# A graph layer and a mixture-of-experts encoder layer on one core: how the attention weights are turned, and how the values' experts are summed

## Chip, cores, metric

The kernel runs on one core of a Trainium2 chip. The metric is the device time of one execution in microseconds. All times below are of the kernel before the change.

## What is computed

The reference is two layers with residuals. The first is a graph convolution over 1250 nodes and 40000 edges. The second is the one that the change touches: a transformer layer over the 1250 nodes with width D = 1024, H = 16 heads of P = 64, and E = 8 experts of which K = 2 are chosen per node and head.

```python
def _gate(x, Wsel):
    s = sigmoid(einsum('bsd,hed->bhse', x, Wsel))
    _, idx = top_k(s, K)
    return s * one_hot(idx, E).sum(-2)

q = rope(einsum('bsd,hdp->bhsp', x, Wq))
k = rope(einsum('bsd,hdp->bhsp', x, Wk))
v = einsum('bsd,bhse,hedp->bhsp', x, _gate(x, Wsel_v), Wv)
att = softmax(einsum('bhsp,bhtp->bhst', q, k) / sqrt(P), axis=-1)
o = einsum('bhst,bhtp->bhsp', att, v)
out = einsum('bhsp,bhse,hepd->bsd', o, _gate(x, Wsel_o), Wo)
```

After it come a layer norm, a feed-forward of 512, and a second layer norm.

## The kernel before

Every fp32 factor is split into a rounded part and a remainder (names ending in hi and lo, or _h and _l), and a product is three matmuls, `dot` at L139 to L141. Nodes are cut into NT = 10 tiles of KT = 125.

The stages in order of time:

- **Graph layer**, 0 to about 314 us. Its normalized output z is turned by `transposed` (L165 to L175) into `zT`, with width on the partitions.
- **Queries and keys**, about 314 to 600 us. `queries_keys` makes, for each of 16 heads, three pieces of columns (L584 scales, L586 to L589 rotate, L590 and L591 split), and writes the split head to DRAM, `kq_d` (L594 the keys, L596 the queries): six DMAs per head on SP's queue. The gates' ten tiles are interleaved. Here a scheduler orders all engines.
- **Values and attention**, about 600 to 2016 us. From here the order of PE's instructions is that in which the code is written; the other engines' is the scheduler's. `values` makes, for head h and tile t, a 125 x 512 product of all eight experts (24 matmuls, with a `yield` after every six), multiplies by the gate on the DVE (L717, `ve`), sums the experts with a reduction (L720, `v`), and splits (L722 on ACT, L723 on POOL). `attention` is a second generator, stepped once in seven of eight yields of `values`. It works by chunks of 256 queries; 16 heads x 5 chunks = 80 chunks.
- **Outputs**, about 2016 to 2890 us. `outputs` loads o (`oc`, L736) and the gates (`gb`, L741), multiplies (L745), splits (L748, L750), multiplies with Wo, and adds to `acc` (L765). The last chunks of attention are stepped beside its beginning.
- **Feed-forward**, to the end.

A chunk of attention has, for each half of 128 queries: queries loaded by POOL's queue (L629), scores `s` of 128 x 1254 by six matmuls (L634), the negated maximum `most` on the DVE (L637), three exponentials on ACT with sums (L642), the total, its reciprocal and the scaling of `p` on the DVE (L645 to L647). Then, five times per chunk, `split`: four PE transposes against the identity turn two tiles of 125 keys into PSUM (L655), ACT rounds them to `att_hi` (L657), and the DVE subtracts to get `att_lo` (L659). `product` multiplies the two with the values (L670, four matmuls of 256 columns for each `split`), and at the end of a chunk o goes out through L676, L677 and L680. Products stand two splits behind.

Weights come through `weights` (L123 the load on SP, L127 the rounding on ACT, L129 the remainder on POOL). The rounded pairs lie in a ring of five slots, the raw blocks in two. SP's queue issues in order, and so does POOL's.

The buffers that matter: `s` one buffer of three PSUM banks, `mm` and `tr` two banks each, `p` five buffers, `q` four, `v2` three, `oc` two.

Of the kernel before, what the change touches and what calls it, by code (L numbers as in the profile page):

```python
# [11 lines left out]
F32 = mybir.dt.float32  # L12
# [10 lines left out]
N = 1250  # L23
# [13 lines left out]
CUT = NZ * KT  # L37
# [33 lines left out]
def gnn_ffn_kernel(  # L71
# [31 lines left out]
    o_d = [dram.tile([P, N], F32, name=f"o_d{j}") for j in range(NP)]  # L103
    g_d = dram.tile([P, N], F32, name="g_d")
# [61 lines left out]
    def transposed(hi, lo, c0, y, psum_tile):  # L166

        for half in range(2):
# [4 lines left out]
            to = (slice(None), slice(4 * half, 4 * half + 4), slice(c0, c0 + KT))  # L173
            nc.scalar.copy(hi[to], p)
            nc.vector.tensor_tensor(lo[to], p, hi[to].bitcast(F32), ALU.subtract)  # L175
# [8 lines left out]
    with ExitStack() as gctx:  # L184
# [16 lines left out]
        with ExitStack() as bctx:  # L201
# [3 lines left out]
            with tc.tile_pool(name="ring1t", bufs=6) as r1:  # L205
                ring += [r1] * 6

                def prepare(t):
# [10 lines left out]
                    transposed(yh, yl, 0, y[:KT], lambda shape: ps.tile(shape, F32, name="tr2", bufs=2))  # L219
# [274 lines left out]
        zT = [[zpool.tile([P, ND, CUT], F32R, name=f"zT0{k}") for k in range(2)]]  # L494
        for t in range(2, NT):
            new = sums([t])
            if t - 2 < NZ:
                transposed(zT[0][0], zT[0][1], KT * (t - 2), zs.pop(0)[:KT], side_bank)
                zs += new
# [5 lines left out]
    def z_of(t, d):  # L505

        k = t if t < NZ else t - NZ
        return [part[:, d, KT * k : KT * (k + 1)] for part in zT[t >= NZ]]

    def rest_of_z():  # L510

        for t in range(NZ, NT):
            z = raws[0].tile([P, D], F32, name="w_raw")[:KT]
            move(z, z_d[t])
            transposed(zT[1][0], zT[1][1], KT * (t - NZ), z, side_bank)
# [3 lines left out]
    def gates(wpool, tmp):  # L519
# [5 lines left out]
        wide = [KT, 2 * H, NX]  # L525
        order = first_wins[:KT, None, :].to_broadcast(wide)

        def pick(chosen, v, m):

            nc.vector.tensor_reduce(m, v, AX.X, ALU.max)  # L530
# [5 lines left out]
        for t in range(NT):  # L536
            p = side_bank([KT, 2 * P])
# [3 lines left out]
            s, a, b, c = (tmp.tile([KT, 2 * H, NX], F32, name=k) for k in ("s", "a", "b", "chosen"))  # L541
            m = tmp.tile([KT, 2 * H], F32, name="m")
# [5 lines left out]
            nc.vector.tensor_tensor(gate_v[:KT, t, :].rearrange("p (h e) -> p h e", h=H), s[:, :H, :], c[:, :H, :],  # L548
                                    ALU.mult)
            nc.vector.tensor_tensor(a[:, H:, :], s[:, H:, :], c[:, H:, :], ALU.mult)  # L550
            pg = psums[-1].tile([P, KT], F32, name="po", bufs=1)
            nc.tensor.transpose(pg, a[:, H:, :].rearrange("p h e -> p (h e)"), ident[:KT, :KT])
            nc.scalar.copy(gT[:, KT * t : KT * (t + 1)], pg)
# [4 lines left out]
    def queries_keys(tab, work):  # L558
# [9 lines left out]
        chunks = [(0, 0, CUT), (1, 0, 376), (1, 376, N - CUT - 376)]  # L568
# [48 lines left out]
    def attention(pool):  # L617
# [46 lines left out]
        def product(h, c, k, parts):  # L664
# [8 lines left out]
            if k + 2 < NT:  # L673
                return
# [252 lines left out]
```

## Time and profile before

| | us |
|---|---|
| median of 3 runs | 3137.41 (3130.07 to 3139.82) |
| profiled execution, its own time | 3137.92 |
| its span, first to last instruction | 3136.1 |
| around the span | 1.8 |
| PE busy | 3023.9 |
| DVE busy | 1957.2 |
| ACT busy | 1098.1 |
| POOL busy | 702.2 |
| PE's weight loads busy (beside the matmuls) | 2554.4 |

A row of the instruction groups reads: line, engine, operation, output<-input, shapes, xcount, then busy us and mean ns of one, then the engine's idle time just before these and who ended it. Matmuls are pipelined, so the mean ns of one is longer than the distance to the next; distances are read from the timeline. A row of the table by stage reads: stretch, its length, then for each engine busy us and number of instructions, the granted TensorE clock, the share of the DMA engines' time and GB/s.

### The profile page before, as it was taken

The page shows a single profiled execution, that of the slowest core. Times are in us where ns is not written, and L with a number is a line of the kernel's source. Part 1 is how long each engine was busy: PE and PEld are TensorE (multiplying, and loading weights), DVE is VectorE, ACT ScalarE, POOL GpSimd, SP SyncE. Part 2 cuts the span into 40 slices and gives each one's busy share as a digit, 9 for nine tenths or more (in the row PEclk, how much of TensorE's full clock was granted, in tenths as well). Part 3 has the DMA queues.
Part 4 walks back from the last instruction along what each step waited for, and adds up shares of the span by engine and source line. Part 5 has one row for each costly group of instructions (what it writes and reads, how often), then busy time and mean ns, then how long its engine had stood idle before and what let it go on. Part 6 is the DMA issues. An engine that isn't in the chain of part 4 may idle for free. (4 is left out here: it accounts for less than half of the span.)

```text
span 3136.1 us, 41143 instructions
## 1 busy us (share of the span) xinstructions
PE 3023.9 (96%) x15618; PEld 2554.4 (81%) x15618; DVE 1957.2 (62%) x3477; ACT 1098.1 (35%) x2472; POOL 702.2 (22%) x570
## 2 busy tenths in 40 slices
PE   6989899999999999999999999899999999999998
PEld 5777889888888888888888888787777777777787
DVE  7965687566666666666666666664444444444685
ACT  5762323234444444444444444431112112111222
POOL 2000334322222122222212222202112112112223
PEclk9999999999999999999999999999999999999999
DMA  3116555612221121222112122434333333333212
GB/s 111 60 41 190 167 142 160 167 43 52 54 55 37 42 52 47 54 55 53 43 39 53 46 54 54 102 94 123 106 85 98 96 85 103 90 82 109 75 41 92
DMA packets 151825, 254.86 MB, mean 81 GB/s; under 512 B 14521, under 2 KB 111801, under 8 KB 151458
## 3 DMA queue, kind: packets, MB, share of 16 engines
q1 hardware_dynamic: 103934, 210.68, 23.9%
q0 software_dynamic: 45824, 31.22, 5.2%
q10 hardware_dynamic: 1860, 10.24, 1.1%
q8 instruction: 124, 2.03, 0.3%
q14 instruction: 83, 0.68, 0.1%
HBM read 200.25 MB, written 56.96 MB: 82 GB/s over the span
## 5 line engine op out<-in xcount | busy, mean ns | idle before, releaser
L129 POOL TENSOR_TENSOR w_lo<-w_raw,w_hi 128x1024 fp32r<-128x1024 f32 x148 | 372.3, 2525 | 1078.0 <-ACT w_hi L127 1069.6
L141 PE MATMUL mm<-w_hi,go_lo 128*125 128x512 f32 x1280 | 507.6, 399 | 24.6 <-DVE go_lo L750 24.5
L139 PE MATMUL mm<-w_hi,go_hi 128*125 128x512 f32 x1280 | 509.5, 398 | 8.8 <-ACT go_hi L748 7.9
L139 PE MATMUL mm<-w_hi,zT 128*125 128x512 f32 x1280 | 508.4, 397 | 4.6 <-ACT raw L584 4.6
L140 PE MATMUL mm<-w_lo,go_hi 128*125 128x512 f32 x1280 | 509.9, 398 | 0.0
L140 PE MATMUL mm<-w_lo,zT 128*125 128x512 f32 x1280 | 507.1, 396 | 0.1
L141 PE MATMUL mm<-w_hi,zT 128*125 128x512 f32 x1280 | 507.1, 396 | 0.0
L642 ACT ACTIVATE p<-s,most 128x416 f32<-128x416 f32 (+1 forms) x480 | 286.0, 605 | 332.8 <-DVE most L637 329.2
L765 DVE TENSOR_TENSOR acc<-acc,mm 125x512 f32<-125x512 f32 x320 | 217.4, 683 | 163.1 <-PE mm L141 163.1
L659 DVE TENSOR_TENSOR att_lo<-tr,att_hi 125x512 fp32r<-125x512 f32 x400 | 262.6, 685 | 88.7 <-ACT att_hi L657 88.6
L141 PEld LDWEIGHTS mm<-w_hi,go_lo 128*125 128x125 f32 x1280 | 239.9, 187 | 93.6 <-DVE go_lo L750 33.7
L748 ACT CAST go_hi<-gb 128x500 fp32r<-128x500 f32 x160 | 98.2, 614 | 602.2 <-PE mm L140 600.6
L657 ACT CAST att_hi<-tr 125x512 fp32r<-125x512 f32 x400 | 235.1, 589 | 179.0 <-PE tr L655 176.0
L139 PEld LDWEIGHTS mm<-w_hi,go_hi 128*125 128x125 f32 x1280 | 239.9, 187 | 68.3 <-ACT go_hi L748 8.2
L745 DVE TENSOR_TENSOR gb<-gb,oc 128x500 f32<-128x500 f32 x160 | 103.8, 690 | 303.0 <-DMA gb<-g_d 301.8
L141 PEld LDWEIGHTS mm<-w_hi,zT 128*125 128x125 f32 x1280 | 238.3, 186 | 60.5
L140 PEld LDWEIGHTS mm<-w_lo,go_hi 128*125 128x125 f32 x1280 | 239.7, 187 | 58.4
L637 DVE TENSOR_REDUCE most<-s 128x1 f32<-128x1254 f32 x160 | 234.2, 1464 | 81.0 <-PE s L634 80.6
L655 PEld LDWEIGHTS tr<-ident,p 128*125 128x125 f32 x1600 | 234.9, 187 | 53.6 <-DVE att_lo L659 18.6
L139 PEld LDWEIGHTS mm<-w_hi,zT 128*125 128x125 f32 x1280 | 239.1, 187 | 41.0 <-ACT raw L584 4.9
L140 PEld LDWEIGHTS mm<-w_lo,zT 128*125 128x125 f32 x1280 | 239.6, 187 | 36.5 <-POOL w_lo L129 0.4
L655 PE MATMUL tr<-ident,p 128*125 128x128 f32 x1600 | 242.0, 274 | 10.2 <-DVE att_lo L659 8.1
(201 smaller groups left out, 5166.6 us busy)
## 6 DMA issues: line engine op xcount, KB each, us to landing
gb<-g_d SPq DMA_DIRECT2D x160, 250.0 KB
w_raw<-in_wv SPq DMA_DIRECT2D x64, 512.0 KB
w_raw<-in_wo SPq DMA_DIRECT2D x64, 512.0 KB
q<-kq_d POOLq DMA_DIRECT2D x160, 128.0 KB, 2.6
kq_d<-qk_hi SPq DMA_DIRECT2D x48, 312.5 KB
kq_d<-qk_lo SPq DMA_DIRECT2D x48, 312.5 KB
k<-kq_d POOLq DMA_DIRECT2D x16, 625.0 KB, 4.4
oc<-o_d SPq DMA_DIRECT2D x80, 125.0 KB
```

The source lines that it names most:

```text
L129: (lo_engine or nc.gpsimd).tensor_tensor(lo, raw, hi.bitcast(F32), ALU.subtract)
L139: nc.tensor.matmul(p, lhsT=lhs[0], rhs=rhs[0], start=start, stop=False)
L140: nc.tensor.matmul(p, lhsT=lhs[0], rhs=rhs[1], start=False, stop=False)
L141: nc.tensor.matmul(p, lhsT=lhs[1], rhs=rhs[0], start=False, stop=stop)
L637: nc.vector.tensor_reduce(most, s[:, :, :KW], AX.XY, ALU.max, negate=True)
L642: nc.scalar.activation(p[:, k0 : k0 + n], s[:, k, :n], AF.Exp, bias=most, accum_out=parts[:, k : k + 1])
L655: nc.tensor.transpose(t[:, j, P * i : P * (i + 1)], p[:, KT * (k + j) : KT * (k + j + 1)], ident)
L657: nc.scalar.copy(hi, t)
L659: nc.vector.tensor_tensor(lo, t, hi.bitcast(F32), ALU.subtract)
L745: nc.vector.tensor_tensor(gb[:, :, mine], gb[:, :, mine], o[:, None, mine].to_broadcast([P, 4, KT]), ALU.mult)
L748: copied = nc.scalar.copy(hi, gb[:, :, mine])
L765: nc.vector.tensor_tensor(acc[t][:, cols], acc[t][:, cols], p, ALU.add)
```

## The change

The softmax of a chunk is no longer turned on PE. Both halves of a chunk go unscaled into one tile `p` of [128, 2, 1280]. Sixteen DMAs from SBUF to SBUF (ten on SP's queue, six on POOL's) move blocks of 32 partitions x 320 columns to `turned`, and two DVE transposes of 32 x 32 blocks finish the turn. The keys are written to DRAM in an order in which these blocks come out as tiles of 128 keys. `split` reads `turned` from SBUF. The division by the sum moves behind the attention: the sums of a head go to DRAM (`r_d`) as reciprocals, and `outputs` loads and multiplies them. Tiles of nodes are 128 instead of 125 for values and gates (the last one 98). The values' experts are summed for two tiles at once with three additions instead of a reduction per tile. PSUM banks: `mm` four, `tr` none. Buffers: `p` one, `turned` two, `q` two, `v2` two, `oc` and `r` one. The schedule of a chunk is rewritten: eight pieces per chunk over three chunks at a time, one piece per yield of `values`.

```diff
-CUT = NZ * KT
+CUT = NZ * P
+NB = 32
+NA = P // NB
+KA = NT * NB
...
@@ queries_keys
-        chunks = [(0, 0, CUT), (1, 0, 376), (1, 376, N - CUT - 376)]
+        chunks = [(0, 0, CUT), (1, 0, 370), (1, 370, N - CUT - 370)]
...
-                    nc.sync.dma_start(kq_d[h][HD * j : HD * (j + 1), 0, :], part[HD:])
+                    to, n, last = kq_d[h][HD * j : HD * (j + 1), 0, :], (NT - 1) * NB, (NT - 1) * P
+                    for a in range(NA):
+                        nc.sync.dma_start(to[:, KA * a : KA * a + n].rearrange("p (b j) -> p b j", j=NB),
+                                          part[HD:, :last].rearrange("p (b a j) -> p b a j", a=NA, j=NB)[:, :, a, :])
+                        nc.sync.dma_start(to[:, KA * a + n : min(KA * (a + 1), N)],
+                                          part[HD:, last + NB * a : min(last + NB * (a + 1), N)])
...
-        interleave(islice(turns, 2), rest, 1, 1 / 3)
+        next(rest)
+        interleave(islice(turns, 2), rest, 1, 2 / 5)
...
@@ attention, softmax
-            p = pool.tile([P, N], F32, name="p", bufs=5)
-            parts = pool.tile([P, 3], F32, name="parts", bufs=4)
+            found = nc.vector.tensor_reduce(most, s[:, :, :KW], AX.XY, ALU.max, negate=True)
             for k, k0 in enumerate(starts):
...
-            total = pool.tile([P, 1], F32, name="total", bufs=4)
-            nc.vector.tensor_reduce(total, parts, AX.X, ALU.add)
+                nc.scalar.activation(p[:, i, k0 : k0 + w], s[:, k, :w], AF.Exp, bias=most,
+                                     accum_out=inverse[h][:, 2 * c + i, k : k + 1])
+            if i == 1:
+                t = turned[n] = pool.tile([P, 2, NA * KA], F32, name="turned", bufs=2)
+                for a in range(NA):
+                    for b in range(NA):
+                        queue = nc.gpsimd if (NA * a + b) % 8 in (2, 5, 7) else nc.sync
+                        queue.dma_start(t[NB * a : NB * (a + 1), :, KA * b : KA * (b + 1)],
+                                        p[NB * b : NB * (b + 1), :, KA * a : KA * (a + 1)])
+            return found.ins
+
+        def sums(h):
+            total = pool.tile([P, 2 * NC], F32, name="total", bufs=2)
+            nc.vector.tensor_reduce(total, inverse.pop(h), AX.X, ALU.add)
             nc.vector.reciprocal(total, total)
-            nc.vector.tensor_scalar_mul(p, p, total)
...
+            nc.sync.dma_start(r_d[h // 2][h % 2].rearrange("(k r) -> r k", r=P), total)
...
@@ attention, split
-            t = side_bank([KT, 2, QW])
-            for j in range(2):
-                for i, p in enumerate(made[h, c]):
-                    nc.tensor.transpose(t[:, j, P * i : P * (i + 1)], p[:, KT * (k + j) : KT * (k + j + 1)], ident)
...
+            x = turned[n].rearrange("p t (A k) -> p (t A) k", A=NA)[:, :, 2 * NB * k : 2 * NB * (k + 1)]
+            hi, lo = (pool.tile([P, 2 * NA, 2 * NB], F32R, name=name, bufs=3) for name in ("att_hi", "att_lo"))
+            nc.scalar.copy(hi, x)
+            nc.vector.tensor_tensor(lo, x, hi.bitcast(F32), ALU.subtract)
...
@@ attention, order of a chunk
+        for n in range(len(chunks) + 2):
+            now, last, before = (0 <= m < len(chunks) for m in (n, n - 1, n - 2))
+            for piece in range(8):
+                if now and piece in (0, 4):
+                    found = softmax(n, piece // 4)
+                if now and piece == 6 and chunks[n][1] == NC - 1:
+                    sums(chunks[n][0])
+                if last and piece == 4:
+                    with tc.issue_after(found) if now else ExitStack():
+                        for i in range(2):
+                            nc.vector.transpose(turned[n - 1][:, i], turned[n - 1][:, i])
+                if before and piece in (0, 1, 2, 3, 5):
+                    product(n - 2, min(piece, 4))
+                if last and piece > 4:
+                    split(n - 1, piece - 5)
+                if before and piece < 2:
+                    split(n - 2, piece + 3)
                 yield
...
@@ values
-                nc.vector.tensor_reduce(v, ve.rearrange("p e k -> p k e"), AX.X, ALU.add)
...
+                        for half in (4, 2):
+                            nc.vector.tensor_tensor(x[:, :, :half], x[:, :, :half], x[:, :, half : 2 * half], ALU.add)
+                        v = pool.tile([P, 2, HD], F32, name="v")[:n, k]
+                        nc.vector.tensor_tensor(v, x[:, :, 0], x[:, :, 1], ALU.add)
...
@@ outputs
-                    o = pool.tile([P, QB], F32, name="oc", bufs=2)
+                    o = pool.tile([P, QB], F32, name="oc", bufs=1)
...
+                    r = pool.tile([P, QB], F32, name="r", bufs=1)
...
+                                nc.sync.dma_start(r[HD * h2 : HD * (h2 + 1), a - QB * c : b - QB * c],
+                                                  r_d[j][h2 : h2 + 1, at_ : at_ + b - a].to_broadcast([HD, b - a]))
+                    nc.vector.tensor_tensor(o, o, r, ALU.mult)
...
-    banks[:] = [2, 2]
+    banks[:] = [4, 0]
```

## Prediction

> **What bounds the kernel now.** I read the engines' totals first, then the table by stage, since the change lies in values and attention (600 to 2120 us):
>
> ```profile
> PE 3023.9 (96%) x15618; PEld 2554.4 (81%) x15618; DVE 1957.2 (62%) x3477; ACT 1098.1 (35%) x2472; POOL 702.2 (22%) x570
> ```
>
> ```profile
> 520.00:570.00 50.00, 50.00 (x263) 46.35 (x262) 32.83 (x54) 16.32 (x28) 26.81 (x17) 1.00 0.66 191
> ...
> 1300.00:1600.00 300.00, 298.89 (x1654) 260.13 (x1653) 200.14 (x298) 130.96 (x342) 72.50 (x81) 1.00 0.20 46
> ```
>
> PE is busy 99.6% of a stretch of attention, at full clock, the DVE 67%, the DMA engines 20%. Queries and keys (first row) are PE's too, but there the DMA engines are at 66%. So time is what PE must issue. That isn't the mean duration of a matmul: they overlap. The timeline gives the distances:
>
> ```profile
> 1202.53 0.39 PE L141 MATMUL mm<-w_hi,zT 128*125 128x512 f32 x1
> 1202.75 0.60 PE L655 MATMUL tr<-ident,p 128*125 128x128 f32 x4
> 1203.11 0.36 PE L670 MATMUL po<-att_hi,v 125*128 125x256 f32 x1
> 1203.31 0.28 PE L670 MATMUL po<-att_lo,v 125*128 125x256 f32 x1
> 1203.43 0.28 PE L670 MATMUL po<-att_hi,v 125*128 125x256 f32 x1
> 1203.54 0.28 PE L670 MATMUL po<-att_lo,v 125*128 125x256 f32 x1
> 1203.66 0.39 PE L139 MATMUL mm<-w_hi,zT 128*125 128x512 f32 x1
> ```
>
> Four transposes take 0.36 us to the first product, and that product's successor starts 0.20 instead of 0.12 us later: 0.44 us for a block of four. The groups, and PE's waits between 660 and 2000 us, for the rest:
>
> ```profile
> L659 DVE TENSOR_TENSOR att_lo<-tr,att_hi 125x512 fp32r<-125x512 f32 x400 | 262.6, 685 | 88.7 <-ACT att_hi L657 88.6
> L655 PE MATMUL tr<-ident,p 128*125 128x128 f32 x1600 | 242.0, 274 | 10.2 <-DVE att_lo L659 8.1 <-DVE total L645 2.1
> L637 DVE TENSOR_REDUCE most<-s 128x1 f32<-128x1254 f32 x160 | 234.2, 1464 | 81.0 <-PE s L634 80.6
> L720 DVE TENSOR_REDUCE v<-ve 125x64 f32<-125x512 f32 x160 | 171.3, 1070 | 8.8 <-DVE ve L717 0.5
> L647 DVE TENSOR_SCALAR p<-p,total 128x1250 f32<-128x1250 f32 x160 | 141.7, 885 | 5.6
> ...
> L586 DVE STREAM_SHUFFLE turned<-raw 128x500 f32<-128x500 f32 x16 | 11.6, 723 | 0.0
> ```
>
> ```profile
> PE tr L655 <- DVE att_lo L659: 5.1, 14, 0.4
> ```
>
> PE waits for nothing but now and then for the DVE to free a transpose bank.
>
> **What the Trainium skill says.** "VectorE: DVE Perf Modes", The three transpose paths: PE's transpose goes to PSUM, the DVE's stays in SBUF and turns only 32 x 32 blocks; so the 16 transfers, which move the blocks, are part of the turn. "Vector Engine (DVE) Microarchitecture Reference", The reshape front-end and per-opcode configuration: the transpose sustains one element per cycle per lane. No row of before has it; the shuffle through the same front end took 723 ns for 500 elements and 583 for 374. "DMA: Bandwidth & Descriptors", Specifications: below 512 B a transfer isn't at line rate, since the engine reads, modifies and writes. The trace has no 128 B store to set against it; its few small packets show no such penalty (168 B in 13 ns, 512 B in 42, 4096 B in 159). Same page, Issuing engines are not separate DMA queues: SP's and POOL's transfers share 16 engines, so the second queue saves issue time alone.
>
> **The change part by part.** Between 800 and 1900 us the timeline has 122 groups of scores, two to a chunk: a chunk takes 18.03 us.
>
> PE. 400 blocks x 0.44 us = **176 us** less, and 8 us of waits for their banks (L655's idle): 184. Products, scores and values keep their numbers and columns (tiles of 128 for 125 change the rows, not the 512 or 256 columns). A chunk becomes 18.03 - 5 x 0.46 = 15.7 us, if nothing else ends it.
>
> DVE per chunk. Now 0.667 x 18.03 = 12.0 us. Off: scaling 2 x 0.885, totals 2 x 0.32, two reductions of 1.07: 4.55. On: two transposes of 1280 elements. By the shuffle's slope (1.11 ns) 1.59 us each; floor 1.33 (one element per cycle at the 0.96 GHz that the first page's Specifications give; an estimate), ceiling 2.8 if fp32 needs two passes; I take 1.55, near L637's 1.46 for 1254: 3.1. Additions of 512, 256 and 128 elements, by L659 (0.69), L677 (0.41) and L548 (0.29), one pair in five halved: 1.46. Sum 12.0 again, but of 15.7: 76%. `att_lo` from SBUF for PSUM: L750 does that in 0.67; nothing.
>
> Its order decides. After the second scores end: `most` 1.47, transposes 3.1, o 0.41, `ve` 0.69, the first `att_lo` 0.69, with handovers some 6.7 us. PE has until its first product: four groups of values (4 x 1.39), a product 0.47, the next scores 1.15: 7.2 us. The slack is half a microsecond. I charge 0.2 us of wait to a chunk, **+16 us**; nothing to 1.9 (transposes of 2.8).
>
> The transfers. Per chunk 16 x 64 runs of 1280 B: 64 runs for each engine. Between the trace's 1000 B (46 ns) and 4096 B (159) a run is some 57 ns, double when contended: 3.7 to 7.3 us of 15.7, over 3.8 us that are there (0.21 x 18). SP issues ten at 0.45 us (its o store, L680), POOL six at 0.57 to 0.74 (L627, L629): 4.5 us, and 2.6 to land (L629): 7 us after the exponentials. The transposes want them 13.8 us after; the next chunk's exponentials, which write the single `p`, 6 to 8 us after, column by column as they were read, and these have 3 us before the next scores need their bank. So covered: 0, with up to 3 us per chunk if a run took three times as long. Behind POOL's six stand `w_lo` and the values' remainder; POOL is at some 8 of 15.7 us, and at a head's boundary I find about 1 us of slack for both. ACT keeps its 8 us.
>
> Keys to DRAM. Per head, SP issues 20 DMAs in place of 6, and 5120 runs of 128 B or less: 320 per engine. At 20 ns (between 13 and 42) 6.4 us, beside 4 us for the queries and 1.5 for weights: 12 us. A head without a gates tile has 13.6 us on PE (72 matmuls at 0.19). Both ends: 13 ns is hidden; 42 ns gives 19 us, 5 too long, 80 us in all; 85 (read and write back) 19 too long, 300 us. The order of the built program matters more: head 13's weights stand on SP behind all 20 stores of head 12, the last of which wait for that head's remainders. From PE's end of head 12: scaling and rotation 4 us, remainders 1.5, stores about 12, the load 3.5, L127 and L129 3.5: some 24 us, PE idle 20. Head 6's are as late, but gates tiles are put there. **+30 us**: 20, and 10 for the heads between.
>
> The rest. Before the first queries, tile 4 of z must now be turned, since its first 12 columns belong to `zT0`: 0 to 6 us, I take 4. In outputs 192 small loads of `r` and 80 products of 250 elements (0.41): SP has 11 us per step for 3 us of issues, the DVE is at 46%, and `oc` in one buffer is filled after L745, still before `gb`, which L745 awaits anyway: 0. Where the last 4.5 chunks lie beside outputs, the DVE has 9.6 + 5.9 us in 15.7: full, +6. Each head's 1280 stores of 4 B (`r_d`) wait for nothing urgent: 0, to 2 us.
>
> Sum: -184 + 16 + 30 + 10 = **-128**, from the profiled execution's 3137.92, which is the median (3137.41) within its spread: **3010 us**.
>
> **Rivals.** (1) *The turn becomes the bound*: transposes at 2.8 us, or transfers landing over 3 us late. The first makes the DVE's chain 9.2 us against 7.2, +2 us on each of 80 chunks, 160: 3155 with the other charges. For it: the order on the DVE is tight, `p` has one buffer. Against: the page's rate, DMA engines at 20%. 0.11. (2) *The small stores bind queries and keys, slower than before*: from 58 ns per run a head takes 23.5 us, +10 on 16 heads, and the gain is gone; at 85 ns 3250. For it: 66% DMA share already in that stretch, two sets of `qk_hi` and `qk_lo` only. Against: the trace's small packets. 0.11. (3) *Half of it arrives*: stalls of 0.8 us a chunk or stores at 42 ns: 3060 to 3090. 0.15. That the transposes stay on PE is excluded: none of L655's is left in the program.
>
> **How the numbers follow.** The forecast has 0.63. What this kernel's measurement can tell from no change is about 0.3%, 9 us. Faster: 0.63 + 0.15 = 0.78; same 0.03; slower 0.19, the part of (1) and (2) beyond that. The low end, 2965, is without the two stalls; 3150 leaves out the worse half of (1) and (2).
>
> **What would show it.** In the changed profile: 1600 fewer PE matmuls, a chunk of 15.7 to 16 us; transposes of 1.4 to 1.6 us; DVE about 76% of an attention stretch; PE's waits for `att_lo` under 30 us. One gap of 20 us in PE near 540 us, ahead of head 13. Wrong if transposes exceed 2.2 us, if ACT's exponentials wait for transfers by microseconds and PE's scores with them, or if queries and keys end after 680 us.

## The result, and the profile after

The changed kernel took **3180.05 us**, the median of 4 runs (3168.78 to 3191.35), beside 3133.74 for the kernel before in the same set of runs: a ratio of 1.0147 (95% interval 1.0104 to 1.019). The forecast was 3010 us, faster. It is slower by 46 us. The profiled execution is the quickest of the four (span 3167.0 us against 3136.1), so the stages below account for 31 us.

The stages, read from the two traces. Queries and keys run from the first scaling of a query to the first score; attention from there to the first product of the outputs; outputs from there to their last product. The last column is the mean over heads 3 to 13.

| us | start | queries, keys | attention | outputs | rest | five chunks of a head |
|---|---|---|---|---|---|---|
| before | 323.4 | 318.7 | 1383.6 | 976.5 | 133.9 | 90.9 |
| changed | 318.9 | 379.2 | 1322.5 | 1015.6 | 130.7 | 84.7 |
| difference | -4.5 | +60.5 | -61.1 | +39.1 | -3.2 | -6.2 |

These boundaries don't cut the two kernels at the same work. Before, the first score comes after 33 groups of six of the values' products, in the changed kernel after 21; and when the outputs start, 7 halves of scores are left before and 4 in the changed kernel. So two other measures are better. Up to the first product of the values, queries and keys take 269.7 us before and 342.8 changed, **73 us** more. (In the rows by stage: engine busy us and instructions for PE, weight loads, DVE, ACT, POOL, then clock, DMA share, GB/s; before, then changed.)

```profile
323.40:593.10 269.70, 253.03 (x1408) 235.82 (x1406) 203.48 (x389) 84.09 (x148) 103.55 (x68) 0.96 0.58 164
318.90:661.70 342.80, 258.22 (x1415) 238.75 (x1414) 192.28 (x389) 84.64 (x148) 99.55 (x67) 0.87 0.64 124
```

And five chunks of a head take 6.2 us less, which is 99 us on 16 heads.

The page's totals of the changed kernel, and its row of granted PE clock by slices:

```profile
PE 2891.7 (91%) x14018; PEld 2395.9 (76%) x14018; DVE 2096.9 (66%) x3400; ACT 1106.8 (35%) x2410; POOL 911.9 (29%) x986
...
PEclk9999999699999999999999999899999999999999
```

The 1600 transposes are gone (15618 matmuls before), and PE is busy 132 us less. But PE no longer fills the span: 91% for 96%. The rows of the table by stage for the two stretches shown of before, in the same columns:

```profile
520.00:570.00 50.00, 38.96 (x208) 36.05 (x206) 21.88 (x49) 10.89 (x21) 9.17 (x9) 0.92 0.69 116
...
1300.00:1600.00 300.00, 287.54 (x1411) 242.21 (x1410) 239.23 (x284) 147.24 (x361) 132.92 (x184) 0.98 0.58 134
```

In attention PE idles 12.5 us of 300, for 1.1 before; the DVE is at 80%, the DMA engines at 58% for 20%. In queries and keys PE stands still for long stretches. What PE waits for, in the list of waits of the whole run (total us, times, longest):

```profile
PE mm L144 <- ACT w_hi L132: 66.9, 3, 54.6
PE mm L146 <- DVE go_lo L801: 52.7, 34, 3.5
PE po L706 <- DVE att_lo L693: 49.9, 31, 8.6
...
PE s L664 <- ACT p L670: 11.7, 6, 4.1
```

Three waits, one in each stage, that weren't there before or were less than half as large (go_lo 24.5 us, att_lo 8.1). The first row is, but for 1 us, two gaps at the weights of queries and keys, 11.3 us at 448 us and 54.6 ending at 614. The timeline of a block of products shows that the saving on PE itself came as forecast: products follow the values' matmuls at once, 0.12 us apart, with no transposes ahead of them:

```profile
1118.87 0.39 PE L146 MATMUL mm<-w_hi,zT 128*128 128x512 f32 x1
1119.10 0.28 PE L706 MATMUL po<-att_hi,v 128*128 128x256 f32 x1
1119.22 0.28 PE L706 MATMUL po<-att_lo,v 128*128 128x256 f32 x1
1119.34 0.28 PE L706 MATMUL po<-att_hi,v 128*128 128x256 f32 x1
1119.46 0.28 PE L706 MATMUL po<-att_lo,v 128*128 128x256 f32 x1
1119.58 0.39 PE L144 MATMUL mm<-w_hi,zT 128*128 128x512 f32 x1
```

The groups of the DVE, shapes kept apart (count, busy us, mean ns, idle before):

```profile
L693 DVE TENSOR_TENSOR att_lo<-turned,att_hi 128x512 fp32r<-128x512 f32 x400 | 313.3, 815 | 160.4 <-ACT att_hi L692 160.2
L729 DVE STREAM_TRANSPOSE turned<-turned 128x1280 f32<-128x1280 f32 x160 | 231.7, 1486 | 0.8 <-DMA o_d<-o 0.8
L762 DVE TENSOR_TENSOR v<-ve 128x64 f32<-128x64 f32 x16 | 55.2, 3450 | 0.0
L762 DVE TENSOR_TENSOR v<-ve 128x128 f32<-128x128 f32 x64 | 18.9, 295 | 6.9 <-DVE ve L760 0.5
```

The transposes take 1.49 us, as assumed. The two odd rows are the others. `att_lo` takes 815 ns on average, for 685 with an input in PSUM, and an addition of 64 elements takes 3450 ns where one of 128 takes 295. The timeline around 1080 us tells why:

```profile
1067.16 4.80 POOL L134 TENSOR_TENSOR w_lo<-w_raw,w_hi 128x1024 fp32r<-128x1024 f32 x2
1067.96 4.09 DVE L762 TENSOR_TENSOR v<-ve 128x64 f32<-128x64 f32 x1
...
1081.48 5.22 DVE L693 TENSOR_TENSOR att_lo<-turned,att_hi 128x512 fp32r<-128x512 f32 x3
...
1082.57 2.37 POOL L134 TENSOR_TENSOR w_lo<-w_raw,w_hi 128x1024 fp32r<-128x1024 f32 x1
...
1085.55 0.39 PE L706 MATMUL po<-att_lo,v 128*128 128x256 f32 x1 [2.06 <-DVE att_lo L693]
```

The addition ends at 1072.05, when GpSimd's two subtractions have ended (1071.96). Three `att_lo` take 5.22 us for 2.0, and PE waits for them. Over the whole trace 17 of the 400 `att_lo` and 15 of the 96 additions last over 1 us, up to 4.0 and 4.1, and every one of them overlaps a `w_lo` on GpSimd. In the kernel before no `att_lo` does (0.69 at most, 400 of 400): it had one input in PSUM. The Trainium skill states it: "SBUF — State Buffer", Who interferes with whom: a DVE instruction with two SBUF inputs contends with a GpSimd instruction that reads SBUF, and one of the two is blocked while the other runs. The trace agrees on the blocking: 103 `att_lo` that run beside GpSimd's DMA issues alone take 693 ns at most. The page adds that the order of issue decides who waits. That is not what the starts show here: 14 of the 17 long `att_lo` start some 1.1 us ahead of the `w_lo` (as at 1081.48 and 1082.57; spans on GpSimd are rough), and end 0.6 us after it. And the addition waited through two subtractions, not one. The reductions (`most`, 1.46 us) and the 32 x 32 transposes (1.49) are as long beside `w_lo` as without.

By chunks, counted from one `most` of a first half to the next, over heads 3 to 13, the five chunks of a head take 16.4, 16.6, 19.8, 16.0 and 15.9 us, where before all take 18.0 to 18.6. The last two are what the prediction forecast for all; in the fifth, PE has no wait at all. The long one is where a new head's four `w_lo` fall.

### The profile page after: what moved, and what is told of

The parts are those of the page before. It is cut to its first block, busy times and chain, and to the rows that moved or that the text cites. A ratio compares the mean times of both kernels' runs of the same rounds, so it can differ in the third digit from the quotient of the medians.

```text
span 3167.0 us, 42077 instructions
## 1 busy us (share of the span) xinstructions
PE 2891.7 (91%) x14018; PEld 2395.9 (76%) x14018; DVE 2096.9 (66%) x3400; ACT 1106.8 (35%) x2410; POOL 911.9 (29%) x986
## 5 line engine op out<-in xcount | busy, mean ns | idle before, releaser
L144 PE MATMUL mm<-w_hi,zT 128*128 128x512 f32 (+1 forms) x1280 | 512.6, 400 | 4.0 <-ACT raw L599 4.0
L145 PE MATMUL mm<-w_lo,zT 128*128 128x512 f32 (+1 forms) x1280 | 513.0, 401 | 1.5 <-POOL w_lo L134 1.2
L146 PE MATMUL mm<-w_hi,zT 128*128 128x512 f32 (+1 forms) x1280 | 511.2, 399 | 0.0
L693 DVE TENSOR_TENSOR att_lo<-turned,att_hi 128x512 fp32r<-128x512 f32 x400 | 313.3, 815 | 160.4 <-ACT att_hi L692 160.2
L692 ACT CAST att_hi<-turned 128x512 fp32r<-128x512 f32 x400 | 231.8, 617 | 191.0 <-PE po L706 87.8
L677 POOL DMA_DIRECT2D turned<-p x480 | 259.0, 546 | 99.6 <-ACT p L670 81.7
L146 PEld LDWEIGHTS mm<-w_hi,zT 128*128 128x128 f32 (+1 forms) x1280 | 241.3, 189 | 61.3
L145 PEld LDWEIGHTS mm<-w_lo,zT 128*128 128x128 f32 (+1 forms) x1280 | 242.0, 189 | 47.3 <-POOL w_lo L134 8.1
L144 PEld LDWEIGHTS mm<-w_hi,zT 128*128 128x128 f32 (+1 forms) x1280 | 241.7, 189 | 43.9 <-ACT raw L599 4.4
L706 PE MATMUL po<-att_lo,v 128*128 128x256 f32 (+1 forms) x800 | 216.8, 292 | 50.2 <-DVE att_lo L693 49.9
L132 ACT CAST w_hi<-w_raw 128x1024 fp32r<-128x1024 f32 x154 | 159.8, 1048 | 233.6 <-DMA w_raw<-in_wo 76.2
```

Of the source, the lines that this page charges most:

```text
L132: nc.scalar.copy(hi, raw)
L144: nc.tensor.matmul(p, lhsT=lhs[0], rhs=rhs[0], start=start, stop=False)
L145: nc.tensor.matmul(p, lhsT=lhs[0], rhs=rhs[1], start=False, stop=False)
L146: nc.tensor.matmul(p, lhsT=lhs[1], rhs=rhs[0], start=False, stop=stop)
L677: queue.dma_start(t[NB * a : NB * (a + 1), :, KA * b : KA * (b + 1)], p[NB * b : NB * (b + 1), :, KA * a : KA * (a + 1)])
L692: nc.scalar.copy(hi, x)
```

## The experiments

All edits are to the changed kernel or, where it is said, to one of these runs. Stages as above, each from the one execution that was profiled; the ratio is to the kernel before in the same set of runs. The sets are e1 to e4, e5 to e8, e9 to e12, e13 to e15.

| run | median us | ratio (95%) | queries, keys | attention | outputs | five chunks |
|---|---|---|---|---|---|---|
| changed | 3180.1 | 1.0147 (1.0104-1.019) | 379 | 1323 | 1016 | 84.7 |
| e1 | 3235.5 | 1.0318 (1.0292-1.0345) | 420 | 1332 | 1023 | 85.6 |
| e2 | 3102.9 | 0.9881 (0.9852-0.9911) | 301 | 1330 | 1018 | 85.4 |
| e3 | 3185.2 | 1.016 (1.0131-1.0188) | 416 | 1290 | 1017 | 82.3 |
| e4 | 3182.8 | 1.0137 (1.0109-1.0165) | 420 | 1291 | 1025 | 82.7 |
| e5 | 3162.7 | 1.0075 (1.0048-1.0102) | 383 | 1326 | 999 | 85.2 |
| e6 | 3194.0 | 1.0173 (1.0142-1.0204) | 299 | 1418 | 1017 | 91.9 |
| e7 | 3162.7 | 1.0077 (1.0054-1.0101) | 371 | 1319 | 1016 | 84.8 |
| e8 | 3112.4 | 0.9907 (0.9879-0.9936) | 379 | 1273 | 1005 | 81.5 |
| e9 | 3200.2 | 1.0215 (1.0192-1.0237) | 301 | 1430 | 1012 | 91.9 |
| e10 | 3031.6 | 0.9684 (0.9662-0.9705) | 297 | 1277 | 1007 | 82.2 |
| e11 | 3181.0 | 1.015 (1.0131-1.0169) | 296 | 1434 | 1003 | 92.4 |
| e12 | 3015.6 | 0.9634 (0.9611-0.9657) | 295 | 1278 | 985 | 82.0 |
| e13 | 3128.2 | 0.9983 (0.9965-1.0002) | 334 | 1323 | 1015 | 85.1 |
| e14 | 3106.8 | 0.9897 (0.987-0.9925) | 389 | 1254 | 1009 | 80.0 |
| e15 | 3062.6 | 0.9766 (0.9747-0.9784) | 294 | 1333 | 978 | 85.5 |

With the small runs of keys as in the changed kernel, the stage of queries and keys took from 379 to 420 us; with plain stores from 294 to 301 in all of them. So savings are taken against runs of the same set. Where a run leaves attention as it is in the changed kernel, attention took from 1319 to 1332 us.

**e1: gb's loads ahead of r's in the code of the outputs.**

```diff
+                    gb = pool.tile([P, 4, QB], F32, name="gb", bufs=2)
+                    ... its two loads, moved up from below r's product
                     o = pool.tile([P, QB], F32, name="oc", bufs=1)
```

> The changed kernel, but in the outputs the two loads of gb are issued on SP ahead of the loads of oc and r. Theory (gb stands on SP behind r, and r waits for the product oc*r, so at each new set of weights gb is issued some 8 us later than before): PE's waits on go_lo fall from 52.7 us to about 25 as in the kernel before, the steps at the 15 changes of weights fall from 14-18 us to 12-13, the outputs take 980 us instead of 1016, and the whole about 3143 us. Rival (the 80 added oc*r products and their stalls beside GpSimd's w_lo cost it, or the added r loads fill the transfers): the outputs stay within 5 us of 1016 and the whole at 3180.

Outputs 1023 us: no gain. But the edit didn't reach SP. At a change of weights its timeline reads as in the changed kernel, `r` ahead of `gb`:

```profile
2556.68 0.33 SPq L785 DMA_DIRECT2D oc<-o_d  x1
2560.46 3.67 SPq L791 DMA_DIRECT2D r<-r_d  x4
2564.24 0.99 SPq L128 DMA_DIRECT2D w_raw<-in_wo  x2
2565.28 1.27 SPq L782 DMA_DIRECT2D gb<-g_d  x2
```

Counted from the start of the outputs, these are the loads of one and the same step: the scheduler still issues a step's `r` ahead of its `gb`, whatever the order in the code. So the run says nothing on its theory; it serves as a repeat of the changed kernel in its set.

**e2: keys stored plain.** This leaves out the keys' order.

```diff
-                    for a in range(NA): ... 8 stores
+                    nc.sync.dma_start(kq_d[h][HD * j : HD * (j + 1), 0, :], part[HD:])
```

> The changed kernel with the keys stored in their plain order, one store for each half as in the kernel before; this leaves out the order of the keys that the turn relies on. Theory (SP issues 20 key stores a head at some 0.66 us each and falls behind PE, and the weights of head 13 stand behind them): the gap of 54.6 us and the one of 11.3 us are gone, the first score starts at about 638 us as before instead of 691, and the whole falls by about 50 us to 3130. Rival (the many 128-byte runs aren't the cause, but the later z tiles or the transfers of the keys at the head of attention are): first score stays after 670 us.

The first score starts at 624.6 us, the gaps are gone, the stage takes 301 us, 119 less than in e1. Up to the first product of the values it takes 269.0 us, as before (269.7). The stores' cost alone turns the whole from slower into faster than before (0.9881).

**e3 and e4: the values' `w_lo` on the DVE, or on GpSimd in quarters.**

```diff
-            w = [weights(wv[h, k]) for k in range(4)]
+            w = [weights(wv[h, k], nc.vector) for k in range(4)]     # e3
+            w = [weights(wv[h, k], pieces=4) for k in range(4)]      # e4
```

> The changed kernel, but w_lo of the values' weights is made by the DVE (some 1.2 us each, 64 of them) and not by GpSimd (2.5 us each). Theory (att_lo now reads both inputs from SBUF, and with GpSimd's subtraction beside it an att_lo takes up to 4.0 us instead of 0.68): no att_lo over 1 us in the attention stage, v<-ve back to 0.3 us, PE's wait on att_lo under 20 us instead of 49.9, the chunk of 20 us in each head falls to about 16, attention is some 60 us shorter and the whole about 3120 us. Rival (the weights themselves come late, because their loads stand on SP behind the transfers): the long chunk stays at 19-20 us, now waiting on w_lo, and the whole at 3180 or later.

> The changed kernel, but GpSimd makes each w_lo of the values in four instructions of 256 columns instead of one of 1024. Theory (a stalled DVE instruction waits for the end of the GpSimd instruction under way, so its stall is as long as that instruction): the longest att_lo falls from 4.0 us to about 1.4, v<-ve from 4.1 to about 1, PE's wait on att_lo from 50 us to 15-25, and the whole by 25 to 50 us. Rival (the two share the path's throughput, or the weights are late): the same stall in sum, and the whole unchanged or longer by GpSimd's added fixed costs.

The groups of e3, `att_lo` and the two homes of `w_lo`:

```profile
L693 DVE TENSOR_TENSOR att_lo<-turned,att_hi 128x512 fp32r<-128x512 f32 x400 | 261.1, 682 | 164.5 <-ACT att_hi L692 164.3
...
L134 POOL TENSOR_TENSOR w_lo<-w_raw,w_hi 128x1024 fp32r<-128x1024 f32 x84 | 216.1, 2590 | 1164.4 <-ACT w_hi L132 916.2 <-DMA x_d<-y 241.7 <-PE mm L145 6.3
L134 DVE TENSOR_TENSOR w_lo<-w_raw,w_hi 128x1024 fp32r<-128x1024 f32 x70 | 84.5, 1207 | 71.2 <-ACT w_hi L132 71.2
```

`att_lo` is back at 682 ns, the addition at 0.27 us (0.29 at most), and the long chunk falls from 19.7 to 17.1. Attention is 1290 us against 1332 in e1: **42 us** (32 against the changed kernel's 1322). The rival, late weights, is refuted: in the changed kernel's attention PE waits for `w_lo` for 1.2 us in all, and the same work on another engine took the stall away. Nor does `w_lo` hold up GpSimd's transfers by much: they start at 1079.31 us, 1.2 after SP's first of the same chunk. In e4 the longest `att_lo` is 1.5 us, as expected of a wait for one short instruction, and attention gains the same 41 us; but 48 `att_lo` are over 1 us, and the additions still reach 4.8 us, as long as six quarters of 0.73 us, so a waiting DVE instruction doesn't get its turn between GpSimd's quarters every time. The 60 us expected of e3 took the long chunk's whole excess for the lock's; the whole times near 3120 didn't come because queries and keys took 416 to 420 us in this set and not 379.

**e5: oc and r held behind the gb of the step before.**

```diff
+                    after = ExitStack()
+                    if gb_loads: after.enter_context(tc.issue_after(gb_loads[-1]))
                     o = pool.tile([P, QB], F32, name="oc", bufs=1)
                     ... loads of o and r
+                    after.close()
```

> The changed kernel, but the loads of oc and r of a step are held behind the load of gb of the step before on SP; in e1_gb_first the same intent left SP's order as it was (r still ahead of gb at each change of weights), so that run repeated the changed kernel and its outputs' 1022 us said nothing of the theory. Theory (gb stands behind r, which waits for the product oc*r): at the 15 changes of weights the two long steps, 12.4 and 15.0 us on average, fall to near the 11.3 and 13.1 of the kernel before, PE's wait on go_lo to about 25 us, the outputs to about 985 us; the rest as in e1_gb_first. Rival (GpSimd's w_lo holds up the added product and go_lo, or oc with one buffer is late by itself): the two steps stay above 26.5 us in sum.

In the changed kernel at a change of weights, SP's queue, the DVE and PE read:

```profile
2494.86 0.33 SPq L779 DMA_DIRECT2D oc<-o_d  x1
2498.79 2.94 SPq L785 DMA_DIRECT2D r<-r_d  x4
2501.84 0.99 SPq L128 DMA_DIRECT2D w_raw<-in_wo  x2
2502.89 1.26 SPq L792 DMA_DIRECT2D gb<-g_d  x2
```

```profile
2496.98 1.78 DVE L787 TENSOR_TENSOR oc<-oc,r 128x250 f32<-128x250 f32 x1 [0.96 <-DVE go_lo L801]
...
2509.67 1.27 DVE L796 TENSOR_TENSOR gb<-gb,oc 128x500 f32<-128x500 f32 x2 [6.91 <-DMA gb<-g_d]
```

```profile
2511.59 0.79 PE L146 MATMUL mm<-w_hi,go_lo 128*125 128x512 f32 x1 [3.49 <-DVE go_lo L801]
```

`r` has one buffer, so its load waits for the product oc * r at 2498.76, which itself takes 1.78 us for 0.42 beside GpSimd's `w_lo`; then come two weights, then `gb`; PE ends up 3.49 us short. With the order mended, outputs take 999 us for 1016 in e7 of the same set, the two long steps 26.2 us in sum for 27.6. Half of the expected gain: PE's wait on go_lo is 38.4 us, not 25. So theory and rival each hold a part; e12 takes GpSimd's part away.

**e6: keys stored plain, put in order by k's load.**

```diff
-                nc.gpsimd.dma_start(keys[h], kq_d[h][:, 0, :].bitcast(F32R))
+                for a in range(NA): ... 2 loads from kq_d's plain columns on nc.gpsimd
```

> The changed kernel with the keys stored in plain order (two stores a head, as before) and put in the turn's order by the load of k, in 8 transfers on GpSimd's queue for each head instead of one. Theory (SP's stores bound queries and keys; in attention GpSimd has the time): the first score at about 630-645 us, no gap over 10 us in queries and keys; in attention one head change costs up to 3 us more, because k lands later; the whole 60 to 80 us under the changed kernel on this chip. Rival (the 5120 runs of 128 bytes are what costs, wherever they stand): the saving is given back at the heads' changes, over 4 us for each head, PE's wait of s on k near 60 us.

Queries and keys are at 299 us. But the chunk at a head's change goes from 16 to 24.6 us, and all of the saving is given back. The timeline at a head's change, GpSimd's queue (its last load of k, then the chunk's transfers) and PE:

```profile
794.33 0.64 POOL L656 DMA_DIRECT2D k<-kq_d  x1
794.90 3.39 POOL L678 DMA_DIRECT2D turned<-p  x6
...
808.99 2.46 PE L665 MATMUL s<-k,q 128*128 128x418 f32 x6 [6.63 <-ACT p L671]
```

It is not k that is late. The eight loads of k take GpSimd from 788.67 to 794.97 us to issue, and the chunk's six transfers stand behind them; the exponentials, which must not overwrite `p` before it is read, wait for those (the last until 808.24), and the next scores for the exponentials. Theory and rival both named a wait on k; part of the price is issue time on a queue, ahead of something urgent. It isn't all of it: GpSimd's transfers here take up to 10.1 us from issue to landing, for 3.1 in the median of the changed kernel, and what delays them isn't shown.

**e7: the key stores on two queues.**

```diff
+                        queue = nc.scalar if a % 2 else nc.sync
```

> The changed kernel with every other pair of key stores on ACT's queue instead of SP's. If SP's issuing (some 0.66 us for a store) is what bounds queries and keys, a head takes SP about 8 us less and the stage falls to PE's time, first score before 650 us. If the small runs' own time on the transfer engines bounds it, the stage gains less than 20 us. If the issuing holds ACT up, with raw and qk_hi behind it, PE waits on raw by tens of us.

371 us for 379 to 383 in the same set: 8 to 12 us gained. The large gap splits into one of 4 to 8 us a head and one of 12.8 at the last; PE's wait for `raw`, by which the third expectation was to be known, is 56.4 us. What holds ACT up is not issuing: its rounding of the next head's `qk_hi` waits for the stores of an earlier head to land (114.5 us, up to 12.8). SP's issue rate alone is not the bound.

**e13: the 20 stores kept, their runs long.** This leaves out the keys' order.

```diff
+                        for c in (slice(KA * a, KA * a + n), slice(KA * a + n, min(KA * (a + 1), N))):
+                            nc.sync.dma_start(to[:, c], part[HD:, c])
```

> The changed kernel with its 20 key and query stores for each head, but the eight key stores of each half take plain column ranges, 288 columns and the rest, so that a run is 1152 bytes and not 128; this leaves out the keys' order. If the number of stores bounds queries and keys (SP's issue time, the completion lanes), the stage stays within 15 us of 380 us and the gap of some 55 us at the weights remains. If the 128-byte runs do, the stage falls to 300-320 us, as with two stores.

334 us, between the two: 55 us below e14 of the same set, and 40 above plain stores (e15, 294). Both count, the short runs for some three parts in five. PE's wait for head 13's weights is halved:

```profile
PE mm L144 <- ACT w_hi L132: 31.7, 2, 28.2
```

Among 480 to 600 us of the changed kernel's trace, a 128 B run takes 13 ns in the median, 16 on average (23 in e7), and the queries' 5000 B runs beside them 386 ns for 260 before: the shortness is paid by the neighbours too.

**e8: one transfer for each chunk instead of 16.** This leaves out the exchange of the blocks.

```diff
-                for a in range(NA): ... 16 transfers
+                nc.sync.dma_start(t, p)
```

> The changed kernel with one transfer of the whole of p into turned for each chunk instead of 16 by blocks (this leaves out the exchange of the blocks, the bytes are the same). Theory (the clean chunks of 15.8 us are PE's own time, and the long ones come from GpSimd's w_lo): the clean chunks stay at 15.8, the long one in each head falls by less than 1.5 us, attention by 5 to 25 us. Rival (the 16 transfers, their issues on SP and GpSimd and the exps that wait for them, are the bound): all chunks fall to about 15.5, ACT's wait of p on turned from 116-155 us to under 30, attention by 60 us or more.

Attention is 1273 us, 46 to 53 less than in e5 and e7, though GpSimd's `w_lo` is still there: the third chunk is 17.6 us. PE's wait on att_lo falls to 20.3 us. So the transfers were not covered, and not the lock's matter alone, though both show in the same chunk; the clean chunks stay at 15.7 to 15.9. The edit takes away the small pieces and fifteen issues at once; what each of them costs isn't taken apart, but e11 will show that issues do cost.

**e14: e8 and e3 together.**

```diff
-            w = [weights(wv[h, k]) for k in range(4)]
+            w = [weights(wv[h, k], nc.vector) for k in range(4)]
...
+                nc.sync.dma_start(t, p)
```

> The changed kernel with w_lo of the values on the DVE and one plain transfer for each chunk (this leaves out the exchange of the blocks). If GpSimd's w_lo and the transfers cost separately, the savings add: attention 1322 - 33 - 50 = about 1240 us, the five chunks of a head 78.5 us in sum, which is PE's own time. If both lie on one path (the transfers make att_lo late and so bring it beside w_lo), attention is 1265-1275 and the five chunks 80.5-81.5 us, no better than with one transfer alone.

Attention 1254 us, the five chunks 80.0: 68 us less than in e13. Alone they take 42 and about 50. So they are mostly separate, and share some 24 us. A likely place is where late transfers push `att_lo` beside `w_lo`: with one transfer (e8) only 4 `att_lo` last over 1 us, for 17. Both expectations missed; the truth lies between. The five chunks are within 1 us of five clean ones (79.3).

The rows of the stage, e13 and then e14, show that a stall costs more than PE's idle time:

```profile
654.20:1976.90 1322.70, 1256.74 (x6168) 1058.23 (x6166) 1028.22 (x1242) 632.29 (x1555) 565.07 (x794) 0.98 0.56 130
711.80:1966.10 1254.30, 1233.40 (x6166) 1050.93 (x6167) 990.45 (x1301) 628.23 (x1556) 169.45 (x268) 0.99 0.53 138
```

Of the 68 us, PE idles 45; in the other 23 it is busy longer with the same products. The granted clock is lower after stalls. By its records (0.984 and 0.994 on average) some 14 of these 23 us are the clock's, an estimate.

**e9: k loaded ahead, a quarter at a time.**

```diff
+            ahead = 2 * c + i - 3
+            if 0 <= ahead < NA and h + 1 < H:
+                with tc.issue_after(asked.ins): load_keys(h + 1, ahead)
```

> As e6_keys_at_load, but the keys of the next head are loaded a quarter at a time during this head's chunks 1 to 3, each behind a q load on GpSimd's queue, and not all at the head's first query. Theory (the 128-byte runs cost nothing where nobody waits for them): first score before 630 us, the chunk at the change of heads back from 24.6 us to about 16.5, attention 1320-1335 us as in the changed kernel, outputs 1016, the whole near 3100 us, faster than before by about 1%. Rival (the runs slow the turn's transfers wherever they stand): the chunks get longer by 1 us or more on average and attention stays over 1400 us.

The head's first chunk is at 15.8 us, as the theory says, but the third is at 26.9. PE's waits:

```profile
PE mm L145 <- POOL w_lo L134: 51.0, 15, 4.9
...
PE mm L144 <- ACT w_hi L132: 24.3, 16, 5.3
```

GpSimd's queue in its third chunk:

```profile
765.62 3.25 POOL L688 DMA_DIRECT2D turned<-p  x6 [1.45 <-ACT p L681]
768.89 2.35 POOL L134 TENSOR_TENSOR w_lo<-w_raw,w_hi 128x1024 fp32r<-128x1024 f32 x1
```

In the changed kernel the third `w_lo` of a head ran ahead of the chunk's transfers (1076.93 against 1079.31). Here it has slid behind them, and PE waits 3.3 to 4.9 us for it in most heads. The rival's figure came, attention over 1400 us, but not for its reason: three of the five chunks are at 15.8 to 15.9 us, the first of them with a quarter of the small runs beside it. The price has moved once more, again 7 us a head, and is again one of GpSimd's order of work.

**e10: e9, e3 and e5 together.**

```diff
+            w = [weights(wv[h, k], nc.vector) for k in range(4)]
...
+                with tc.issue_after(asked.ins): load_keys(h + 1, ahead)
...
+                        after.enter_context(tc.issue_after(gb_loads[-1]))
```

> The keys ahead of time (e9_keys_ahead), w_lo of the values on the DVE (e3_wlo_dve) and oc and r behind gb (e5_r_after_gb) together. If the three costs are separate, the savings add: queries and keys 299 us, attention about 1290, outputs about 998, the whole some 3045 to 3065 us, 2.5% faster than before. If they share one cause (the load of the transfer engines, say), the sum is clearly less, the whole above 3090.

3031.6 us, 3.2% faster than before and better than the expected sum: with `w_lo` off GpSimd, e9's new wait is gone too, and attention takes 1277 us. The order of the loads is worth less here than in e5: outputs take 1007 us, for 1012 in e9 without it.

**e11: e10 with all transfers on SP.**

```diff
-                        queue = nc.gpsimd if (NA * a + b) % 8 in (2, 5, 7) else nc.sync
+                        queue = nc.sync
```

> e10_three_mended with all 16 transfers of a chunk issued by SP. If GpSimd's queue (6 transfers, q, v2's low half and now k in order, each behind the exps) is what makes the remaining long chunks, attention falls by 15 us or more and PE no longer waits on v2. If SP's 16 issues of some 0.6 us (10 us of a chunk) bring the last transfers later, ACT's exps wait longer for turned and attention rises by 10 us or more.

```profile
ACT p L681 <- DMA turned<-p: 338.2, 179, 8.4
```

Attention 1434 us, 157 more. The exponentials, which write the single `p`, wait for the transfers that read it; in e10 they do so for 129.8 us. The second queue is worth 10 us a head.

**e12: e10 with all of the outputs' low halves on the DVE.**

```diff
-                w = [weights(wo[j, 4 * half_e + i], nc.vector if j == 0 and i % 2 == 0 else None) for i in range(4)]
+                w = [weights(wo[j, 4 * half_e + i], nc.vector) for i in range(4)]
```

> e10_three_mended with the low halves of all the outputs' weights made by the DVE too. If GpSimd's subtraction beside oc*r and go_lo (1.6-1.7 us instead of 0.42 and 0.67 at a change of weights) makes what is left of the long steps, the outputs fall from 998 to 980 us or below. If the loads' order and landing make it, or the DVE now waits for w_hi in its own queue, the outputs stay within 5 us or get longer.

**3015.6 us, 0.9634 of before** (0.9611 to 0.9657), the fastest of all. Outputs fall from 1007 to 985 us, PE's wait on go_lo from 47.1 to 22.5. The groups of e12, to compare with 860 ns for go_lo and 830 for oc in the changed kernel:

```profile
L817 DVE TENSOR_TENSOR go_lo<-gb,go_hi 128x500 fp32r<-128x500 f32 x160 | 109.9, 687 | 0.1
L802 DVE TENSOR_TENSOR oc<-oc,r 128x250 f32<-128x250 f32 x80 | 36.3, 454 | 111.0 <-DMA oc<-o_d 84.0 <-issue 15.3 <-DMA r<-r_d 6.9
```

**e15: e12 with the low half of v2 on the DVE.**

```diff
-                        nc.gpsimd.tensor_tensor(v2[:, :, HD:], v, ...)
+                        nc.vector.tensor_tensor(v2[:, :, HD:], v, ...)
```

> e12_mended_wo_dve with the low half of v2 on the DVE too. If PE's wait on v2 (14.5 us) is GpSimd's queue, with the subtraction behind k's and p's transfers, it goes and the whole falls by about 10 us to 3005. If something else is late at the same place, the wait moves there and the whole stays.

```profile
PE po L717 <- DVE v L776: 47.6, 15, 6.8
```

47 us slower than e12. The wait moved, and grew: on the DVE's in-order queue the subtraction stands behind longer work than on GpSimd's. One of them has its input at 745.87 us and runs at 749.70, behind a `w_lo`, a `most` and a transpose. In attention, 55 us longer than in e12, PE idles 32 us more, and is busy 24 us longer with the same products at a clock of 0.98 for 1.00.

## Why the prediction was wrong

**PE's own saving: right.** A block of transposes less was to make a chunk 15.7 us; clean chunks take 15.8 to 15.9. Were all like that, five would take 79.3 us, and 16 heads (90.9 - 79.3) x 16 = 186 us less. They take 84.7: 99 us less. The other 87 are, but for some 11, two terms that the prediction set at nothing: with both taken away, in e14, five chunks take 80.0, and (80.0 - 79.3) x 16 = 11.

**"`att_lo` from SBUF for PSUM: L750 does that in 0.67; nothing": wrong, 32 to 42 us** (e3 against the changed kernel and e1). It is the kind of the inputs that counts, not the duration of the instruction when alone. The trace of before showed it in the very row that was named, whose mean isn't 0.67:

```profile
L750 DVE TENSOR_TENSOR go_lo<-gb,go_hi 128x500 fp32r<-128x500 f32 x160 | 131.7, 823 | 2.4 <-ACT go_hi L748 2.2
```

823 ns on average over a median of 0.67 us is a tail: 26 of these 160 last over 1 us, up to 2.88, and all 26 overlap a `w_lo`. I took the typical value and left the tail. The same reading undoes the three additions, costed at 0.69, 0.41 and 0.29: the last of them reaches 4.1 us. The reduction that they replace, with one input, was never over 1.11.

**"So covered: 0" for the transfers: wrong, about 50 us** (e8). The bound that I gave, up to 3 us a chunk, held it: 50 us are 0.6 a chunk. The exponentials do wait for the transfers (115.7 us in all, 83 times, up to 5.7), and PE's scores for the exponentials (11.7), which I had called the sign of an error. An issue on SP takes 0.59 us for the 0.45 charged, and a run of 1280 B 80 ns in the median for 57, so the last transfers land later. Rival (1) had the transfers as one of its two ways to the slower side, but with 3 us a chunk as the point from which they count, as if a lesser lateness were free. It is free only while every chunk is like the clean ones; where `w_lo`, `att_lo` and the transfers meet, in a head's third chunk, there is no slack left.

**"+30" for the keys: the mechanism and its place right, the size wrong.** Head 13's weights stand behind head 12's stores; the gap was forecast at 20 us near 540 and is 54.6 at 559. Head 6's weights, for which no gap was forecast because gates tiles stand there, are late by 11.3. Up to the first product of the values the cost is 73 us, and against plain stores in the same set the stage is 80 to 119 longer (e6 and e8, e15 and e14, e2 and e1). The term was costed as 20 ns for each run, and that was not far off (13 in the median, 16 to 23 on average). Three things were left out: the number of stores costs by itself (e13), the queries' longer runs beside them slow down, and lateness adds up from head to head. A head's stores were given 12 us, under PE's 13.6; they take SP 14 to 19, mostly 16 to 18, so SP falls behind with each head until the weights that stand behind the stores are missed. Between the two sets of weights PE loses nothing (heads 7 to 12 start within 75 us, for 81 before), so the 10 us charged to the heads between were not spent there. Rival (2) named this stage, but through the time of a run, 58 ns and more; rival (3) named stalls in the chunks *or* dearer stores, and both came.

**"0" for the outputs: wrong, 39 us.** I argued that a buffer less for `oc` was harmless because `gb` is awaited anyway. But loads on SP go in order: `oc` and `r`, with one buffer each, make `gb` wait for the product of the step before. Of the added time e5 took away some 18 us, by the order alone (in e10 some 5), and e12 another 22 against e10, by taking GpSimd off. In the steady steps (11.2 us, as before) my argument holds; it fails at the changes of weights, where the queue holds two or four weights as well.

**The smaller terms.** The DVE's order, +16: it costs a clean chunk nothing, since PE never waits in it; the 0.15 us that clean chunks are over 15.7 are PE's own, an error of the forecast's prices. That 12 us of them lie near the 16 is luck. Tile 4 of z, +4: not seen, the first queries start 4.5 us earlier. The end of attention beside outputs, +6: when the outputs start, 4 halves of scores are left for 7 before, yet the first five steps take 100 us for 101.5; so this overlap got dearer by more than 6 us. No run takes it apart; it stays open, as does why the small stores' stage varies from 379 to 420 us between sets.

Of the signs named ahead: 1600 matmuls fewer, transposes of 1.49 us, clean chunks and the large gap at head 13 came, with a smaller one at head 6; PE's wait on att_lo of 49.9 us, instead of under 30, and the exponentials' waits told of the two terms that failed. Queries and keys ended at 661, under the 680 that I had set as a limit.

## What to carry to other kernels

Moving an input of a DVE instruction from PSUM to SBUF is not free while GpSimd reads SBUF: look for the tail, the distance between mean and median, of a row with the same kind of inputs, and put the two kinds of work on one engine or apart in time. Count issues and run lengths for each queue and stage, and ask for every buffer that is taken away which load in program order stands behind it. When a change has moved the bound off an engine, its costs can be mended one by one, but check where each mended wait goes: the repair of the keys won nothing by itself (e6, e9), and together with the others it made the changed kernel 3.7% faster than the one before.

## What the runs showed of the hardware

- A two-input subtraction or addition on the DVE lasts up to 4.1 us (5.8 in e8) instead of 0.3 to 0.7 beside GpSimd subtractions of 2.5 us, when both inputs are in SBUF; with one in PSUM never over 0.69, in 47 `att_lo` of the kernel before that lie beside such a subtraction. Cutting GpSimd's instruction into quarters shortens the longest `att_lo` from 4.0 to 1.5 us but lets an addition wait up to 4.8.
- The 32 x 32 transposes of [128 x 1280] in fp32 take 1.486 us, 1.16 ns an element, and reductions 1.46, both untouched by GpSimd's `w_lo` (30 and 31 of 160 lie beside one).
- PE's granted clock fell to 0.50 in the gap of 54.6 us (580 to 600 us) and was 0.66 over the ten microseconds in which one of 4.0 us ended:

```profile
580.00:600.00 20.00, 0.00 (x0) 0.00 (x0) 0.04 (x1) 0.50 (x1) 0.84 (x1) 0.50 0.68 114
660.00:670.00 10.00, 8.35 (x24) 6.61 (x25) 4.01 (x5) 1.07 (x2) 5.13 (x4) 0.66 0.80 103
```

So the lower mean clock of the changed kernel (0.964 for 0.985) follows its gaps; with most of the gaps gone it is 0.983 in e12. A stall is paid twice, once idle and once in slower products after it, as e13 against e14 and e15 against e12 show.
